# The second experts' stage of a graph-network kernel: row gathers, weight loads, column widths and the last two units rearranged

## The chip, the cores and the metric

The kernel runs on one core of a Trainium2 chip. The time is device time in microseconds (us) of one execution; a kernel's time is the median of several runs. All times of one execution below are counted from the start of its span.

## What is computed

The reference is two rounds of graph aggregation plus attention, each followed by a mixture of experts, over 1250 nodes of 1024 features. The change touches only the last step, the second mixture:

```
scores = einsum('btd,ed->bte', x, gate_w)            # 8 experts
topk_scores, topk_idx = top_k(scores, 2)
topk_probs = softmax(topk_scores)
h1, h2 = split(einsum('btd,ehd->bteh', x, w12))      # 256 + 256 columns per expert
hidden = silu(h1) * h2
expert_out = einsum('bteh,edh->bted', hidden, w3)
y = sum over the two chosen experts of probability * expert_out
```

The kernel's output is x + y, where x in y is the layer-normed x.

## The kernel before, in words

Everything but the last stage is the same in both kernels and is left out here. The framework in which it is written records the instructions, lets a scheduler order them per engine by its own estimates, and inserts the semaphores; a block under a condition is scheduled as one piece.

The last stage computes only what the routing chose. Each node's two experts are known only on the chip, so the nodes of an expert are packed into **units** of up to four blocks (UC = 4) of 128 nodes. There are NU = 12 units; the first five are always run, the others only if their count is at least 1. Lines 1151 to 1296 work out, on the chip, for every unit the expert (`unit_e`), the number of nodes (`taken`), the row numbers for gathers (`idx`, for whole rows of the first unit; `idx_q`, for quarters of rows of the others; `idx_s`, for scatters) and the weights (`gate`).

For one unit the work is:

- **weights** (`load_unit`, L1304): w12 (2 MB) and w3 (1 MB) of its expert, from SyncE's DMA queue for units from 3 on and the first load of unit 0, from ScalarE's queue for units 1 and 2. Each has three buffers.
- **rows**. For unit 0, GpSimd gathers whole rows, 128 at a time (L1320, tile `xe`), TensorE transposes them (L1342) and ScalarE and VectorE in turn evict them (L118 and L120, called by `evac`) into `xeT`. For the other units, GpSimd gathers quarters of rows (`fetch`, L1345 to L1356, tile `xq`, two buffers, four gathers for a block of 128 nodes), and VectorE turns them into `xeT` (`turn`, L1374).
- **gate and up** (`gate_up`, L1381 to L1392), twice, once for each 128 of the 256 hidden columns: 8 matmuls into `p1`, 8 into `p2`, Silu on ScalarE (L1389), the product on VectorE (L1390) into `hT` (named `h3T`), and a memset of the rest of a block of 128 (L1392).
- **down** (L1398 to L1418): for each block, four matmuls (L1406), the eviction with the weight (L1409 on ScalarE, L1411 on VectorE, tile `ye`), and a scatter that adds the rows to the output in memory (L1412, GpSimd).

How many columns a matmul has depends on the unit's count, which is known only at run time. `by_width` (L193) therefore writes the work out once for each width, as the **arms** of a binary tree of jumps, and every engine jumps by the count that it loaded (L1323, `number`). Gate and up had seven arms (L53: 128, 192, 256, 320, 384, 448, 512 columns), rows and down have four (L54, `COUNTS`: 128, 256, 384, 512).

The loop (L1360) runs over the units: in unit u it states the fetch of unit u + 2, the weights of u + 1, gate and up, the turn of u + 1, and down. A unit from 5 on stands under its own condition (`when`, L1328). So three queues matter: GpSimd's, which holds gathers and scatters in one order, ScalarE's, which holds evictions and the weights of units 1 and 2, and SyncE's. The order on each is the scheduler's: in the kernel before, GpSimd has the fetch of unit 1, one row gather of unit 0, the fetch of unit 2, the three other row gathers, the fetch of unit 3, the scatters of unit 0, and from there mostly a fetch and a scatter in turn; the fetches of units 8 and 9 stand behind the scatters of units 5 and 6.

Of the kernel before, what the change touches and what calls it, by code (L numbers as in the profile page):

```python
# [22 lines left out]
P = 128  # L23
N = 1250
D = 1024
KB = D // P
# [23 lines left out]
UC = 4  # L50
NU = 12
COLS = NU * UC
WIDTHS1 = [128, 192, 256, 320, 384, 448, 512]  # L53
COUNTS = [P * (c + 1) for c in range(UC)]  # L54
LN_EPS = 1e-5
EXACT = 4096.0
# [48 lines left out]
def network(tc: tile.TileContext, a: dict, out: bass.AP, env: SimpleNamespace, exact: bool):  # L105
    nc = tc.nc
    wpool, small, psum = env.wpool, env.small, env.psum
    ident, eps_t, iota8 = env.ident, env.eps_t, env.iota8
# [6 lines left out]
    def evac(dst, src):  # L115
        turn[0] += 1
        if turn[0] % 2:
            nc.scalar.copy(dst, src)  # L118
        else:
            nc.vector.tensor_copy(dst, src)  # L120

    def bank(name):
        return psum.tile([P, 512], F32, name=name, tag="bank")
# [69 lines left out]
    def by_width(n, widths, work):  # L193

        if len(widths) == 1:
            return work(widths[0])
        m = len(widths) // 2
        with tc.If(n <= widths[m - 1]) as cmp:
            by_width(n, widths[:m], work)
        with cmp.Else():  # L200
            by_width(n, widths[m:], work)
# [106 lines left out]
    with tc.tile_pool(name="edges", bufs=1, side="right") as edp, \  # L308
# [5 lines left out]
        with tc.tile_pool(name="mix0k", bufs=1, side="right") as kp, ExitStack() as s_edges:  # L314
            blocks = iter(())
            for half in range(2):
# [40 lines left out]
                coming = iter([(pair, j) for pair in range(4) for j in range(nj)])  # L357
# [92 lines left out]
    with tc.tile_pool(name="wo0", bufs=1) as bp:  # L450
# [21 lines left out]
        if not exact:  # L472
            most1 = bp.tile([P, 1], F32, name="most1")
            nc.vector.tensor_reduce(most1, most, AX.X, OP.max)
            pt = bank("pmost")
# [6 lines left out]
    if not exact:  # L482
        with tc.tile_pool(name="deg", bufs=1) as dp:
# [7 lines left out]
            pt = bank("pdc")  # L491
# [78 lines left out]
    hn, b = gcn_features(0)  # L570
# [5 lines left out]
    hn, b = gcn_features(1)  # L576
# [5 lines left out]
    taken = rp.tile([1, E], I32, name="taken")  # L582
    with tc.tile_pool(name="route0a", bufs=1) as ra, tc.tile_pool(name="route0w", bufs=2) as rw:
# [175 lines left out]
        pt = bank("ptab")  # L759
# [22 lines left out]
        pt = bank("pspread")  # L782
# [21 lines left out]
    with s_route:  # L804
        quarters = x1n_d.rearrange("n (j f) -> (n j) f", j=4)
        with tc.tile_pool(name="moe0", bufs=1) as mp:
# [45 lines left out]
            xeT = first_columns()  # L852
            ws = weights(0)

            number = [nc.values_load(taken[0:1, e:e + 1], min_val=0, max_val=CAP) for e in range(E)]
# [445 lines left out]
    with tc.tile_pool(name="moe1", bufs=2) as ep:  # L1301
        SP, ACT = mybir.EngineType.SP, mybir.EngineType.Activation

        def load_unit(w, which, queue):  # L1304
            queue.dma_start(w[0], a["L1_ffn_w12"][bass.ds(which, 1)].rearrange("e (p k) f -> p (e k) f", k=KB))
            queue.dma_start(w[1], a["L1_ffn_w3"][bass.ds(which, 1)].rearrange("e (k p) f -> p (e k) f", p=P))

        def places():
            return (wpool.tile([P, KB, 2 * H1], F32, name="w12", tag="w"),
                    ep.tile([P, H1 // P, D], F32, name="w3", bufs=3))  # L1310

        def expert_of(u, engine):
            return nc.values_load(unit_e[0:1, u:u + 1], engines=(engine,), min_val=0, max_val=E - 1)

        ws = places()
        load_unit(ws, expert_of(0, SP), nc.sync)

        xe = ep.tile([P, UC, D], F32, name="xe1", bufs=1)
        for c in range(UC):
            nc.gpsimd.indirect_dma_start(  # L1320
                out=xe[:, c], out_offset=None, in_=env.x3n_d,
                in_offset=bass.IndirectOffsetOnAxis(ap=idx[:, c:c + 1], axis=0))
        number = [nc.values_load(taken[0:1, u:u + 1], min_val=0, max_val=UC * P) for u in range(NU)]  # L1323

        queues = [(nc.sync, SP) if u > 2 else (nc.scalar, ACT) for u in range(NU)]
        which = [None] + [expert_of(u, queues[u][1]) for u in range(1, NU)]

        def when(u, work):  # L1328

            if u < 5:  # L1330
                return work()
            with tc.If(number[u] >= 1):
                work()

        xeT = ep.tile([P, KB, UC * P], F32, name="xeT1")

        def turn_first(n):
            for c in range(n // P):
                for b0 in (0, 4):
                    pt = bank("pte1")  # L1340
                    for b in range(4):
                        nc.tensor.transpose(pt[:, b * P:(b + 1) * P], xe[:, c, b0 + b::KB], ident)  # L1342
                    evac(xeT[:, b0:b0 + 4, c * P:(c + 1) * P], pt.rearrange("p (b q) -> p b q", b=4))

        def fetch(u):  # L1345
            xq = ep.tile([P, UC * 4, B, KB], F32, name="xq1")

            def work(n):
                for i in range(n // B):
                    nc.gpsimd.indirect_dma_start(  # L1350
                        out=xq[:, i].rearrange("p c b -> p (c b)"), out_offset=None, in_=quarters3,
                        in_offset=bass.IndirectOffsetOnAxis(
                            ap=idx_q[:, i % 4, u * UC + i // 4:u * UC + i // 4 + 1], axis=0))

            when(u, lambda: by_width(number[u], COUNTS, work))
            return xq  # L1356

        by_width(number[0], COUNTS, turn_first)
        coming = [fetch(1)]
        for u in range(NU):  # L1360
            later = u + 1 < NU
            if u + 2 < NU:
                coming.append(fetch(u + 2))
            if later:
                xq = coming.pop(0)
                xeT2 = ep.tile([P, KB, UC * P], F32, name="xeT1")
                ws2 = places()
            w12, w3 = ws
            hT = ep.tile([P, H1 // P, UC * P], F32, name="h3T")

            def turn(n):
                for c in range(n // P):
                    i0, i1 = 4 * c, 4 * c + 4
                    nc.vector.transpose(xeT2.rearrange("p b (i r) -> p i b r", r=B)[:, i0:i1],  # L1374
                                        xq[:, i0:i1].rearrange("p i c b -> p i b c"))

            def unit():
                if later:
                    when(u + 1, lambda: load_unit(ws2, which[u + 1], queues[u + 1][0]))
                for i in range(H1 // P):  # L1380
                    def gate_up(n):  # L1381
                        m = -(-n // P) * P
                        p1, p2 = bank("p1"), bank("p2")
                        for pw_, off in ((p1, 0), (p2, H1)):
                            for k in range(KB):
                                nc.tensor.matmul(pw_[:, :n], w12[:, k, off + i * P:off + (i + 1) * P], xeT[:, k, :n],  # L1386
                                                 start=(k == 0), stop=(k == KB - 1))
                        sg = ep.tile([P, UC * P], F32, name="sg1")
                        nc.scalar.activation(sg[:, :n], p1[:, :n], AF.Silu)  # L1389
                        nc.vector.tensor_mul(hT[:, i, :n], sg[:, :n], p2[:, :n])  # L1390
                        if n < m:
                            nc.vector.memset(hT[:, i, n:m], 0.0)  # L1392

                    by_width(number[u], WIDTHS1, gate_up)
                if later:
                    when(u + 1, lambda: by_width(number[u + 1], COUNTS, turn))

                def down(n):  # L1398
                    sent = []
                    for c in range(n // P):  # L1400
                        ye = ep.tile([P, D], F32, name="ye1", bufs=6)
                        own = gate[:, u * UC + c:u * UC + c + 1]
                        for half in range(2):
                            py = bank("py1")
                            for i in range(H1 // P):
                                nc.tensor.matmul(py, hT[:, i, c * P:(c + 1) * P], w3[:, i, half * 512:(half + 1) * 512],  # L1406
                                                 start=(i == 0), stop=(i == H1 // P - 1))
                            if half:
                                nc.scalar.activation(ye[:, 512:], py, AF.Copy, scale=own)  # L1409
                            else:  # L1410
                                nc.vector.tensor_scalar(ye[:, :512], py, own, None, op0=OP.mult)  # L1411
                        add = nc.gpsimd.indirect_dma_start(  # L1412
                            out=out, out_offset=bass.IndirectOffsetOnAxis(
                                ap=idx_s[:, u * UC + c:u * UC + c + 1], axis=0),
                            in_=ye, in_offset=None, bounds_check=N - 1, oob_is_err=False, compute_op=OP.add)
                        for other in sent:
                            tc.declare_no_dep(add.ins, other.ins, reason="no token is twice at an expert")
                        sent.append(add)  # L1418

                by_width(number[u], COUNTS, down)  # L1420

            when(u, unit)
            if later:
                xeT, ws = xeT2, ws2
    s_moe.close()


# [47 lines left out]
```

## Time and profile before

| what | value |
|---|---|
| median of 3 runs | 3457.25 us (3454.84 to 3459.14) |
| the profiled execution | 3460.19 us |
| its span | 3458.5 us |
| TensorE busy | 3249.1 us, 94% |
| GpSimd busy | 635.5 us, 18% |
| VectorE busy | 941.7 us, 27% |
| end of the routing work (`idx_q`, L1289) | 3110.5 us |
| first gate matmul (L1386) | 3152.0 us |
| last down matmul (L1406) ends | 3433.6 us |
| gate and up matmuls, idle before them for "issue" | 16.8 us |
| down matmuls, idle before them for "issue" | 8.9 us |

In the profile's groups a line has: source line, engine, operation, output and inputs, shapes and count; then busy time and mean ns of one; then the engine's idle time just before and what ended it. "PE" is TensorE, "DVE" VectorE, "ACT" ScalarE, "POOL" GpSimd. "issue" is time in which an engine waited for nothing that the profile shows. In the chain and the timeline a line begins with its start and its length in us. An fp32 matmul of the program shows as two records.

### The profile page before, as it was taken

The page shows a single profiled execution, that of the slowest core. Times are in us where ns is not written, and L with a number is a line of the kernel's source. Part 1 is how long each engine was busy: PE and PEld are TensorE (multiplying, and loading weights), DVE is VectorE, ACT ScalarE, POOL GpSimd, SP SyncE. Part 2 cuts the span into 40 slices and gives each one's busy share as a digit, 9 for nine tenths or more (in the row PEclk, how much of TensorE's full clock was granted, in tenths as well). Part 3 has the DMA queues.
Part 4 walks back from the last instruction along what each step waited for, and adds up shares of the span by engine and source line. Part 5 has one row for each costly group of instructions (what it writes and reads, how often), then busy time and mean ns, then how long its engine had stood idle before and what let it go on. Part 6 is the DMA issues. An engine that isn't in the chain of part 4 may idle for free.

```text
span 3458.5 us, 30927 instructions
## 1 busy us (share of the span) xinstructions
PE 3249.1 (94%) x11696; PEld 1969.2 (57%) x11696; DVE 941.7 (27%) x2405; ACT 358.1 (10%) x622; POOL 635.5 (18%) x543
## 2 busy tenths in 40 slices
PE   6999999999999699999699999999999999986887
PEld 3474656554557466756355555447777454653553
DVE  4248335531114623231520000111111111341221
ACT  1001011100004111111110011000000000000000
POOL 0006786042001041210200000110000010005431
PEclk9999999999998599999899999999999999987998
DMA  4715222054104155554620000220100110236652
GB/s 154 170 58 131 25 1 25 25 182 149 47 31 152 48 185 189 168 182 118 217 101 25 25 25 25 91 108 1 35 15 25 61 48 18 97 119 197 186 171 51
DMA packets 147616, 317.95 MB, mean 92 GB/s; under 512 B 38951, under 2 KB 60366, under 8 KB 143884
## 3 DMA queue, kind: packets, MB, share of 16 engines
q1 hardware_dynamic: 82108, 216.85, 18.4%
q0 software_dynamic: 40240, 48.25, 7.0%
q10 hardware_dynamic: 24992, 49.16, 4.7%
q8 instruction: 174, 2.85, 0.3%
q14 instruction: 102, 0.84, 0.1%
HBM read 239.25 MB, written 77.82 MB: 92 GB/s over the span
## 4 chain that ended last, share of the span: by engine, by line
PE 52%; DMA 2%; issue 1%; DVE 1%; ACT 0%; POOL 0%; another core or an unknown queue 0%; POOLq 0%; DVEq 0%; ACTq 0%; SPq 0%
PE ppn L166 8%; PE pqT L941 8%; PE pa L515 5%; PE p L1386 5%; PE ph L166 4%; PE pwo L166 4%; PE ph L1065 4%; PE pv L166 3%; PE py L1406 2%; PE py L889 2%; PE pgate L869 2%; PE pup L869 2%; PE psc L1083 1%; DMA res_d<-xt 1%; PE pkv L1000 1%
## 5 line engine op out<-in xcount | busy, mean ns | idle before, releaser
L277 POOL DMA_INDIRECT adj_d<-cnt,cell x167 | 261.3, 1565 | 91.9 <-issue 41.7
L1386 PE MATMUL p<-xeT,w 128*128 128x384 f32 (+4 forms) x640 | 167.6, 425 | 18.0 <-issue 16.8
L190 POOL TENSOR_TENSOR xr<-xr,bo 128x512 f32<-128x512 f32 (+1 forms) x40 | 50.4, 1264 | 711.9 <-PE pwo L166 453.5
L1386 PEld LDWEIGHTS p<-xeT,w 128*128 128x128 f32 x640 | 113.8, 201 | 73.9 <-issue 35.5
L869 PE MATMUL pgate<-xeT,wg 128*128 128x392 f32 (+3 forms) x512 | 152.4, 452 | 2.7 <-DVE ye L892 2.5
L166 PE MATMUL pqk<-wk,x0T 128*128 128x512 f32 (+1 forms) x320 | 144.8, 607 | 9.2 <-ACT x0T L118 6.9
L889 PE MATMUL py<-hT,wdb 128*128 128x392 f32 (+3 forms) x512 | 145.8, 444 | 4.1 <-ACT wdb L879 4.0
L166 PE MATMUL pv<-wv,x1T 128*128 128x512 f32 (+1 forms) x320 | 144.3, 609 | 4.2 <-ACT x1T L118 2.2
L869 PE MATMUL pup<-xeT,wu 128*128 128x392 f32 (+3 forms) x512 | 148.2, 443 | 0.0
L166 PE MATMUL ph<-ws,h1T 128*128 128x512 f32 (+1 forms) x320 | 143.2, 596 | 0.0
L166 PE MATMUL pqk<-wq,x0T 128*128 128x512 f32 (+1 forms) x320 | 140.7, 594 | 0.0
L166 PE MATMUL ppn<-wn,x1T 128*128 128x256 f32 (+1 forms) x640 | 138.8, 379 | 0.0
L1065 PE MATMUL ph<-x1T,ws 128*128 128x416 f32 (+1 forms) x384 | 138.2, 512 | 0.0
L166 PE MATMUL pv<-wv,x0T 128*128 128x512 f32 (+1 forms) x320 | 138.0, 593 | 0.0
L166 PE MATMUL ph<-wgcn,x0T 128*128 128x512 f32 (+1 forms) x320 | 138.0, 593 | 0.0
L166 PE MATMUL pwo<-wo,attn0T 128*128 128x512 f32 (+1 forms) x320 | 137.7, 593 | 0.1
L166 PE MATMUL ppn<-wn,h1T 128*128 128x512 f32 (+1 forms) x320 | 137.7, 592 | 0.0
L166 PE MATMUL pwo<-wo,attn1T 128*128 128x512 f32 (+1 forms) x320 | 137.5, 593 | 0.0
L941 PE MATMUL pqT<-x1T,wk 128*128 128x416 f32 (+1 forms) x384 | 135.6, 512 | 0.0
L941 PE MATMUL pqT<-x1T,wq 128*128 128x416 f32 (+1 forms) x384 | 135.6, 512 | 0.0
L166 PEld LDWEIGHTS ppn<-wn,x1T 128*128 128x128 f32 (+1 forms) x640 | 120.1, 188 | 17.7
L869 PEld LDWEIGHTS pgate<-xeT,wg 128*128 128x128 f32 x512 | 99.4, 195 | 50.5 <-issue 6.4
(384 smaller groups left out, 4474.8 us busy)
## 6 DMA issues: line engine op xcount, KB each, us to landing
wg<-in_L_ffn_gate_w_dram SPq DMA_DIRECT2D x8, 2048.0 KB
wu<-in_L_ffn_up_w_dram SPq DMA_DIRECT2D x8, 2048.0 KB
w<-in_L_ffn_w_dram SPq DMA_DIRECT2D x8, 2048.0 KB
wd<-in_L_ffn_down_w_dram SPq DMA_DIRECT2D x7, 2048.0 KB
y_d<-ye ACTq DMA_DIRECT2D x30, 416.0 KB
adj_d<-ezero SPq DMA_DIRECT2D x2, 6105.0 KB
res_d<-xr SPq DMA_DIRECT2D x45, 256.0 KB
table<-adj_d ACTq DMA_DIRECT2D x36, 312.5 KB
```

Of the source, the lines that this page charges most:

```text
L166: nc.tensor.matmul(pr[:TS[t], :cols], xT[:, k, TOK[t]], w[:, k, :], start=(k == 0), stop=(k == nk - 1))
L190: nc.gpsimd.tensor_add(xr[:TS[t]], xr[:TS[t]], bias[:TS[t]])
L277: nc.gpsimd.indirect_dma_start(out=adj_d[e % 2], out_offset=bass.IndirectOffsetOnAxis(ap=cell[:, e:e + 1], axis=0), in_=cnt[:, e:e + 1], i ...
L515: nc.tensor.matmul(pa, edges if by_node else feats, feats if by_node else edges, start=(s == 0 and i == 0), stop=(s == T - 1 and i == len( ...
L869: nc.tensor.matmul(pw[:, :n], w[:, k, ic], xeT[:, k, :n], start=(k == 0), stop=(k == KB - 1))
L889: nc.tensor.matmul(py[:, :n], wdb[:, i, b, :], hT[:, i, :n], start=(i == 0), stop=(i == I0 // P - 1))
L941: nc.tensor.matmul(pq[:, :n], w[:, k, pair * P:(pair + 1) * P], xT[:, k, c0:c0 + n], start=(k == 0), stop=(k == KB - 1))
L1000: nc.tensor.matmul(pkv[:, :P], kf[:TS[t], t, :], v[:TS[t], t, pair * P:(pair + 1) * P], start=(t == 0), stop=(t == T - 1))
L1065: nc.tensor.matmul(ps[:, :n], w[:, k, q0 + f * P:q0 + (f + 1) * P], xT[:, k, c0:c0 + n], start=(k == 0), stop=(k == KB - 1))
L1083: nc.tensor.matmul(pl[:ts, :E], xnt[:, k, :ts], gw[:, k, :], start=(k == 0), stop=(k == KB - 1))
L1386: nc.tensor.matmul(pw_[:, :n], w12[:, k, off + i * P:off + (i + 1) * P], xeT[:, k, :n], start=(k == 0), stop=(k == KB - 1))
L1406: nc.tensor.matmul(py, hT[:, i, c * P:(c + 1) * P], w3[:, i, half * 512:(half + 1) * 512], start=(i == 0), stop=(i == H1 // P - 1))
```

## The change

It has four parts, all in the last stage.

1. Every weight load of a unit is kept in program order, which bars the scheduler from moving it ahead. The load of the counts (`number`) on GpSimd is put behind the last row gather of unit 0, and with it all fetches.
2. The rows of unit 0 are always turned in all four blocks, not by the count.
3. Gate and up use the four widths of `COUNTS` in place of the seven, so hT is always filled to a whole block and the memset goes.
4. The loop becomes a function. Unit 11 stands inside unit 10's condition, so that one jump passes both.

```
-WIDTHS1 = [128, 192, 256, 320, 384, 448, 512]
...
         def load_unit(w, which, queue):
-            queue.dma_start(w[0], a["L1_ffn_w12"][bass.ds(which, 1)].rearrange("e (p k) f -> p (e k) f", k=KB))
-            queue.dma_start(w[1], a["L1_ffn_w3"][bass.ds(which, 1)].rearrange("e (k p) f -> p (e k) f", p=P))
+            for part, name, order in ((w[0], "w12", "e (p k) f -> p (e k) f"), (w[1], "w3", "e (k p) f -> p (e k) f")):
+                tc.keep_in_program_order(queue.dma_start(
+                    part, a["L1_ffn_" + name][bass.ds(which, 1)].rearrange(order, p=P)))
...
         for c in range(UC):
-            nc.gpsimd.indirect_dma_start(
+            whole = nc.gpsimd.indirect_dma_start(
...
-        number = [nc.values_load(taken[0:1, u:u + 1], min_val=0, max_val=UC * P) for u in range(NU)]
+        with tc.issue_after(whole.ins):
+            number = [nc.values_load(taken[0:1, u:u + 1], min_val=0, max_val=UC * P) for u in range(NU)]
...
-        def turn_first(n):
-            for c in range(n // P):
-                for b0 in (0, 4):
+        for c in range(UC):
+            for b0 in (0, 4):
...
-        by_width(number[0], COUNTS, turn_first)
-        coming = [fetch(1)]
-        for u in range(NU):
+        def units_from(u, xeT, ws, coming):
...
                     def gate_up(n):
-                        m = -(-n // P) * P
...
-                        if n < m:
-                            nc.vector.memset(hT[:, i, n:m], 0.0)
-
-                    by_width(number[u], WIDTHS1, gate_up)
+
+                    by_width(number[u], COUNTS, gate_up)
...
                 by_width(number[u], COUNTS, down)
 
+                if later and u == NU - 2:
+                    units_from(u + 1, xeT2, ws2, coming)
+
             when(u, unit)
-            if later:
-                xeT, ws = xeT2, ws2
+            if later and not (u == NU - 2):
+                units_from(u + 1, xeT2, ws2, coming)
+
+        units_from(0, xeT, ws, [fetch(1)])
```

In the changed program GpSimd has the four row gathers first, then the fetches of units 1, 2 and 3; from there its order is as before. ScalarE has unit 1's w12 behind its last row eviction, unit 1's w3 behind the first Silu of unit 0, unit 2's w12 behind the second, and unit 2's w3 behind unit 0's evictions. VectorE turns unit 1 between the two products of unit 0, where it did so ahead of both.

More of the change, by code (lines that the diff above doesn't have):

```diff
@@ L1335, in network @@
         xeT = ep.tile([P, KB, UC * P], F32, name="xeT1")
-        def turn_first(n):
-            for c in range(n // P):
-                for b0 in (0, 4):
[L1340 to L1343, printed above, removed]
+        for c in range(UC):
+            for b0 in (0, 4):
+                pt = bank("pte1")
+                for b in range(4):
+                    nc.tensor.transpose(pt[:, b * P:(b + 1) * P], xe[:, c, b0 + b::KB], ident)
+                evac(xeT[:, b0:b0 + 4, c * P:(c + 1) * P], pt.rearrange("p (b q) -> p b q", b=4))
         def fetch(u):
```

## The prediction

> **What bounds the kernel now.** The page's slices come first: TensorE is busy nine tenths of nearly every slice, but the last five of 40 (from 3026 us) show 8, 6, 8, 8 and 7.
>
> ```profile
> PE   6999999999999699999699999999999999986887
> PEclk9999999999998599999899999999999999987998
> ```
>
> The granted clock falls there too. Next, the chain that ended last, in order of time, through the stage that the diff touches (columns: start, length, what):
>
> ```profile
> 3126.25 2.93 issue
> 3129.18 0.23 POOLq L1323
> 3129.41 10.78 DMA xe<-x3n_d,idx
> ...
> 3143.41 5.58 DMA xe<-x3n_d,idx
> 3149.03 1.99 PE pte L1342 x8
> ...
> 3151.99 17.46 PE p L1386 x64
> 3169.45 10.36 PE py L1406 x24
> ...
> 3275.70 3.57 PE p L1386 x32
> 3279.27 4.04 issue
> 3283.31 5.47 PE p L1386 x32
> ```
>
> Two things are seen. The first gate matmul waits for the first unit's rows until 3151.99, though their indices (L1274) are ready at 3108.50: GpSimd first issues twelve fetches of unit 1 (from 3111.48), then one row gather, eight fetches of unit 2, and three more row gathers. From then TensorE carries the chain to 3433.6, but in narrow units it stops for "issue", and the half of matmuls after such a stop runs slow (5.47 against 3.57). Third, the groups by shape, which give the widths that ran:
>
> ```profile
> L1386 PE MATMUL p<-xeT,w 128*128 128x384 f32 x256 | 83.7, 487 | 2.9 <-issue 2.9
> L1386 PE MATMUL p<-xeT,w 128*128 128x448 f32 x64 | 24.2, 539 | 0.0
> L1386 PE MATMUL p<-xeT,w 128*128 128x192 f32 x128 | 23.1, 343 | 5.3 <-issue 5.0 <-DVE ye L1411 0.3
> L1386 PE MATMUL p<-xeT,w 128*128 128x128 f32 x128 | 19.0, 320 | 8.8 <-issue 8.8
> L1386 PE MATMUL p<-xeT,w 128*128 128x320 f32 x64 | 17.5, 434 | 1.0 <-DVE xeT L120 1.0
> ```
>
> A unit has 64 of these, so by the timeline units 0 to 9 run 320, 384, 192, 448, 128, 384, 192, 128, 384, 384 columns; units 10 and 11 are empty. The timeline also gives the side path of the second half, from GpSimd's fetch for unit 8 to its matmuls:
>
> ```profile
> 3340.41 0.94 POOL L1350 DMA_INDIRECT xq<-x3n_d,idx_q  x1 [5.06 <-DMA out_dram<-ye,idx_s]
> ...
> 3357.54 5.83 DVE L1374 STREAM_TRANSPOSE xeT<-xq 128x1024 f32<-128x1024 f32 x3 [0.77 <-DMA xq<-x3n_d,idx_q]
> ```
>
> **Rows first.** In the changed program's order GpSimd issues the four row gathers before it loads any count. It is idle then (its wait for idx_q is 27.9 us), so they start at about 3108.7 and take 4 x 1.25 us (0.95 and 0.30 of issue). In the trace a row gather reaches the transposes 4.5 to 5.6 us after its start, and a second of the same burst 2.2 us later (3146.83, 3149.03); so the fourth is there at 3108.7 + 4.7 + 3 x 2.2 = 3120.0. It is turned in 2.0 and evicted in 0.7, with 0.5 of issue: the first gate matmul at 3123.2. This contains the fourth block, now always turned (2.2 us). Bounds: 3120 if GpSimd's pace alone counts, 3128 if weights of unit 0 slow the gathers. **-28.8**.
>
> What is moved behind: unit 1's fetches now start at 3114.2 instead of 3111.48, are issued by 3129 and turned by 3140.5; unit 1 needs them at 3154.6. Unit 2's are turned by 3149.5, and unit 0's DVE evictions wait for that, 5.4 us after the down matmuls start; in unit 1 the like wait was 8.7 us (3201.5 to 3210.2) and cost TensorE 0.27. On ScalarE's queue unit 1's w12 moves from 3100.8 to behind the last row eviction (3122.5), its w3 and unit 2's w12 behind unit 0's two Silus (3128 and 3139), and unit 2's w3 behind unit 0's evictions (3154). Unit 3's w12, issued at 3169.49, has its last packet by 3178, so 8.5 us each: unit 1's is there 20 us early. On SyncE unit 0's w3 moves ahead of two branch trees. All at nothing; without that cover each us late is a us.
>
> **Four widths.** 320 becomes 384, 192 becomes 256 twice, 448 becomes 512. 64 matmuls of 384 take 20.9 us, of 448 24.05, of 320 17.46, so 64 columns cost 3.5: units 0, 2, 3, 6 pay 14.1 in all. The eight memsets (0.11 each) leave VectorE, off the path: 0.
>
> **What the fewer arms give back.** Without stops and at full clock (5.36 for 32 of 192, 3.73 for 32 of 128, 0.442 for a down matmul) units 2, 4, 6, 7 would take 17.8, 11.0, 17.8, 11.0 us; they took 25.5, 22.4, 23.4, 19.6: 33 us over. Two jumps explain it. I count the built programs' TensorE instructions (one fp32 matmul is two loads and two multiplies: 640 records for 320 matmuls). An arm is 64 of them, and from one half's arm to the next half's it was some 400 instructions, now some 200. In the trace's branch records 14 of 18 jumps of 350 and more last 1.2 to 6.5 us, and none of the 12 shorter ones lasts over 0.45. After the change the longest jump that runs is 333, the others 304 at most. Wide units hid most of it (5.93 us showed as 0.81 in unit 1).
>
> [...]
> Unit 1 -0.8; unit 2 from 25.5 to 17.8 + 3.5 + 0.5 = 21.8: -3.7; unit 4 from 22.4 to 14.0: -8.4; units 0 and 3 +3.5 each; unit 5 unchanged.
>
> **What is late next.** Units 6 and 7 could lose 10, but unit 8's rows are fetched behind unit 5's scatter-adds. From unit 5's end (3329.4) the fetch ends at +23.2, the rows are turned from +28.1 to +34.0, and nothing in that is TensorE's. VectorE does that turn between unit 7's two products (the order is kept), so unit 7's down matmuls follow it (4 us, clock low again) and unit 8 starts at +38.5, against +43.0: **-4.5**. Unit 9's rows (turned at +60.7 in the trace) then meet unit 8's second product at +59.4: unit 8 gives back 1.0 net of its 0.5 stop. Unit 9: 0.
>
> **One jump.** At the end GpSimd, which finishes last, skips unit 10, adds to its semaphores, skips unit 11 and does so again: 1.8 us between in its records, now gone; TensorE's two skips (3.4 and 5.5 us) lie beside that. **-1.8**.
>
> Sum: -28.8 + 3.5 - 0.8 - 3.7 + 3.5 - 8.4 - 4.5 + 1.0 - 1.8 = -40.0. Against the profiled execution, 3460.19 (span 3458.5 and 1.7 around it), that is 3420; it lies 2.9 above the median of 3457.25, so the median becomes 3417, and I say 3418.
>
> **Rivals.**
> 1. [...] 14%.
> 2. Stops gone wholly, and the fetch chain of unit 8 gives way, since scatter and fetch meet less traffic (5.06 of it was a wait for a landing). Then units 4, 6 and 7 give 2.6 and 6 more, with 1.0 in unit 8: 3407. 18%.
> 3. [...] 3%.
> That the rows do not go ahead is ruled out by the order of GpSimd's instructions.
>
> **Numbers.** The likeliest case, 3418, has 62%, with 3409 to 3429 of its own (3 us on the rows, 4 on the stops, 3 on unit 8). 3% lie near the old time. A measurement tells some 0.2%, 7 us, from no change. The range 3402 to 3438 takes in the likeliest case and the second rival and leaves out the first and third. Faster 94%, same 3%, slower 3%.
>
> **What would show it.** First gate matmul near 3123 (right if 3120 to 3128); only shapes 128, 256, 384, 512 in the gate row; its "issue" idle near 5 instead of 16.8; unit 4 in about 14 us; unit 8's start 38 to 39 us after unit 5's end, with its turn just before. Wrong if the chain shows issue gaps of 4 us in units 4 and 7, or a weight load ahead of unit 1.

## The result and the profile after

| what | before | after |
|---|---|---|
| median of the runs, same chip | 3457.57 us (4 runs) | 3425.07 us (4 runs, 3415.3 to 3425.5) |
| ratio, 95% interval | | 0.990 (0.9881 to 0.9919) |
| profiled execution, its span | 3460.19, 3458.5 | 3425.42, 3423.7 |
| index cast (`idx`, L1274 / L1273) | 3108.3 | 3103.1 |
| index cast to first gate matmul | 43.7 | 15.0 |
| index cast to the end of the span | 350.2 | 320.6 |

The change saves 32.5 us. The prediction said 39 to 40. In the slices of the span (tenths, 40 slices) the last five of TensorE now read 9, 6, 9, 8, 7:

```profile
PE   6999999999999789999699999999999999996987
PEclk9999999999998689999899999999999999997998
```

The groups by shape show the four widths and what TensorE still waits for ahead of them:

```profile
L1383 PE MATMUL p<-xeT,w 128*128 128x384 f32 x320 | 108.7, 502 | 9.2 <-DVE ye L1406 5.3 <-issue 3.9
L1401 PE MATMUL py<-w,h3T 128*128 128x512 f32 x200 | 91.4, 611 | 7.1 <-DVE h3T L1387 6.3 <-issue 0.8
L1383 PE MATMUL p<-xeT,w 128*128 128x256 f32 x128 | 28.1, 380 | 0.6 <-DVE ye L1406 0.6
L1383 PE MATMUL p<-xeT,w 128*128 128x512 f32 x64 | 27.6, 592 | 0.0
L1383 PE MATMUL p<-xeT,w 128*128 128x128 f32 x128 | 14.6, 275 | 0.0
```

"issue" idle is 3.9 for gate and up (16.8 before) and 0.8 for down (8.9 before). In its place stand two waits for VectorE that were not there: 5.3 for `ye` and 6.3 for `h3T`. TensorE's timeline says where (start, length, what, in brackets the idle time before it):

```profile
3118.14 20.81 PE L1383 MATMUL p<-xeT,w 128*128 128x384 f32 x64
3138.78 10.60 PE L1401 MATMUL py<-w,h3T 128*128 128x512 f32 x24
3154.69 23.53 PE L1383 MATMUL p<-xeT,w 128*128 128x384 f32 x64 [5.31 <-DVE ye L1406]
...
3251.52 7.31 PE L1383 MATMUL p<-xeT,w 128*128 128x128 f32 x64
3258.66 3.60 PE L1401 MATMUL py<-w,h3T 128*128 128x512 f32 x8
3266.12 22.42 PE L1383 MATMUL p<-xeT,w 128*128 128x384 f32 x64 [3.86 <-issue]
...
3335.02 5.49 PE L1401 MATMUL py<-w,h3T 128*128 128x512 f32 x6 [6.34 <-DVE h3T L1387]
3340.30 21.11 PE L1383 MATMUL p<-xeT,w 128*128 128x384 f32 x64
```

Each wait costs twice: 64 matmuls of 384 columns take 20.81 undisturbed, but 23.53 behind the wait of 5.31 and 22.42 behind that of 3.86, and six down matmuls take 5.49 where 2.65 is their pace. The granted clock gives the sizes: it was 0.73 of full speed in the 10 us from 3154.69 (2.7 us lost), 0.84 in the 10 us from 3266.12 (1.6) and 0.50 over those six down matmuls (2.6), and 1.00 in the undisturbed 20.81. VectorE's timeline has the cause of the first wait:

```profile
3139.06 0.55 DVE L1387 TENSOR_TENSOR h3T<-sg,p 128x384 f32<-128x384 f32 x1 [1.31 <-PE p L1383]
3142.77 2.03 DVE L1372 STREAM_TRANSPOSE xeT<-xq 128x1024 f32<-128x1024 f32 x1 [3.15 <-DMA xq<-x3n_d,idx_q]
3150.68 2.01 DVE L1372 STREAM_TRANSPOSE xeT<-xq 128x1024 f32<-128x1024 f32 x1 [5.88 <-DMA xq<-x3n_d,idx_q]
3152.61 2.03 DVE L1406 TENSOR_SCALAR ye<-py,gate 128x512 f32<-128x512 f32 x3
```

Unit 0's three evictions (`ye`) stand behind the turn of unit 2, which waits for rows twice (3.15, 5.88). They start 13.8 us after the down matmuls, and unit 1's first matmul waits for them. That it waits for the PSUM tiles which they empty (the matmuls' outputs take turns in eight of them, `bank`) is read from the program; the profile names only `ye`. GpSimd had fetched these rows late:

```profile
3125.05 0.95 POOL L1350 DMA_INDIRECT xq<-x3n_d,idx_q  x1 [0.31 <-issue]
3130.97 0.94 POOL L1350 DMA_INDIRECT xq<-x3n_d,idx_q  x1 [4.98 <-DMA xq<-x3n_d,idx_q]
3132.35 0.94 POOL L1350 DMA_INDIRECT xq<-x3n_d,idx_q  x1 [0.44 <-issue]
```

After unit 1's twelve fetches it waits 4.98 us for a landing before it starts on unit 2's eight. The kernel before had such a wait behind the same twelve fetches, and then took 1.37 us for each of the eight instead of 1.25:

```profile
3125.30 0.95 POOL L1350 DMA_INDIRECT xq<-x3n_d,idx_q  x1 [0.30 <-issue]
3129.41 0.94 POOL L1320 DMA_INDIRECT xe<-x3n_d,idx  x1 [3.16 <-DMA xq<-x3n_d,idx_q]
```

From first gate matmul to first gate matmul (the two profiles' timelines, us; unit 9 to the end of its down matmuls, which before is 3435.3; the 3433.6 of the first table is where the chain leaves TensorE):

| | before | after | difference | predicted |
|---|---|---|---|---|
| index cast to unit 0 | 43.7 | 15.0 | -28.6 | -28.8 |
| unit 0 | 27.7 | 36.6 | +8.9 | +3.5 |
| unit 1 | 32.6 | 34.6 | +2.0 | -0.8 |
| unit 2 | 25.3 | 20.8 | -4.5 | -3.7 |
| unit 3 | 38.0 | 41.5 | +3.5 | +3.5 |
| unit 4 | 22.5 | 14.6 | -7.9 | -8.4 |
| unit 5 | 31.2 | 32.7 | +1.5 | 0 |
| units 6 and 7 | 43.0 | 41.5 | -1.5 | -4.5 |
| unit 8 | 31.8 | 31.4 | -0.4 | +1.0 |
| unit 9 | 31.3 | 31.2 | 0 | 0 |
| to the end | 23.2 | 20.8 | -2.4 | -1.8 |
| stage | 350.2 | 320.6 | -29.6 | -40.0 |

The other 5.2 us of the profiles' difference lie ahead of the index cast, where both kernels have the same instructions. Four kernels of sets three and four (below), with the same work there, have the cast between 3102.6 and 3110.2, so this is scatter and no part of the change. In sets one and two it comes at 3114.3 to 3124.6.

### The profile page after: what moved, and what is told of

Read it like the earlier page. It is cut to its first block, busy times and chain, and to the rows that moved or that the text cites. A ratio compares the mean times of both kernels' runs of the same rounds, so it can differ in the third digit from the quotient of the medians.

```text
span 3423.7 us, 30825 instructions
## 1 busy us (share of the span) xinstructions
PE 3254.8 (95%) x11704; PEld 1966.0 (57%) x11704; DVE 941.5 (27%) x2398; ACT 359.2 (10%) x623; POOL 635.7 (19%) x543
## 5 line engine op out<-in xcount | busy, mean ns | idle before, releaser
L1383 PE MATMUL p<-xeT,w 128*128 128x384 f32 (+3 forms) x640 | 179.0, 442 | 9.8 <-DVE ye L1406 5.9
```

## The experiments

There were four sets of runs, each on one chip with the kernel before beside it: the first on one chip, the second and third on another, the fourth on a third. In the first two sets the kernel before took 3487.2 and 3483.6 us, in the last two 3459.0 and 3460.3. In the first two every profile shows long waits that the others lack (below, "The standstill"); times are compared only within a set, or between sets three and four and the recorded runs.

**Rows first, alone** (set 1; the kernel before with these edits):

```
-        number = [nc.values_load(...) for u in range(NU)]
+        with tc.issue_after(whole.ins):
+            number = [nc.values_load(...) for u in range(NU)]
...
-        by_width(number[0], COUNTS, turn_first)
```

and the weights in program order and all four blocks of unit 0 turned, as in the change.

> The kernel before with the first two parts of the change alone: rows ahead of fetches and weights, four blocks always turned; seven widths and two jumps stay. Theory: the first gate matmul comes 15 us after the index cast in place of 43.7, so 28.6 are gained there; VectorE's turn of unit 2 (late rows) again stands ahead of unit 0's evictions and, as unit 0 is 3.5 us shorter at 320 columns, TensorE waits 5 to 9 us for ye; the issue stops of units 2, 4 and 7 stay. So 3434 to 3438, first gate matmul 28 to 29 earlier against the index cast. Rival (the wait for ye belongs to the wider columns or to the shorter code, not to the order of the rows): no wait for ye, and the whole 28.6 is seen: 3429.

Measured: 3466.7, ratio 0.9944 (0.9925 to 0.9964). TensorE had turned the rows 17 us behind the index cast (43 in the kernel with one jump alone, same set), but then stood still for 18.2 us:

```profile
3127.55 3.92 PE L1343 MATMUL pte<-ident,xe 128*128 128x128 f32 x19 [0.35 <-issue]
3149.68 20.24 PE L1386 MATMUL p<-xeT,w 128*128 128x320 f32 x64 [18.21 <-issue]
```

Neither theory had this, and neither is settled here: with such a standstill in front, the rows had time to come, and no wait for `ye` is longer than 0.28. That the kernel is 20.5 us below the one before, about what the theory said, is luck, since 18.2 us of standstill are in it and others in its neighbour. The stops of units 2, 4 and 7 stayed, as the theory said.

**Four widths, alone** (set 1):

```
-                    by_width(number[u], WIDTHS1, gate_up)
+                    by_width(number[u], COUNTS, gate_up)
```

> The kernel before with the four widths alone. Theory (stops sit on jumps between arms that are far apart): units 0 and 3 +3.5 each, unit 2 25.4 to about 21, unit 4 22.4 to about 14.5, units 6 and 7 together 43.0 to about 41.5, no wait for ye over 1 us: -6 to -8 in all, 3450. Rival (the stops stay however long the jumps are): 14 more columns' time and no gain, 3471. A second rival (nothing but the wait for the rows at the stage's start and GpSimd's chain sets the end, so that shorter units are waited away): within 3 us of before.

Measured: 3467.7, ratio 0.9946 (0.9928 to 0.9964), so 12 to 25 us less: more than the theory, far from both rivals. Against the kernel with one jump alone, from the same set, unit 2 takes 21.7 for 26.2, unit 3 41.5 for 38.0, unit 4 14.7 for 21.8, and units 6 and 7 42.2 for 49.2. The last pair is what the expectation missed: it had been sized by the stops of one profile (43.0), and stops vary.

**The changed columns with the long code** (set 1, and again in set 2):

```
                     def gate_up(n):
+                        n = -(-n // P) * P
...
-                    by_width(number[u], COUNTS, gate_up)
+                    by_width(number[u], WIDTHS1, gate_up)
```

> The changed kernel with the seven-armed tree, but every arm rounded up to whole blocks of 128 columns: the columns computed are those of the changed kernel, the length of the code and of its jumps that of the kernel before. Theory: the stops come back with the length alone: issue idle of the gate row from 4 to about 15 us, unit 2 from 20.9 to 26 or 29, unit 4 from 14.5 to about 22, unit 8 starts up to 1.5 later; 3437 to 3444. Rival (the stops went for another cause than the length of the jumps): 3425, issue idle near 4.

Measured in set 1: 3473.1, ratio 0.997 (0.9959 to 0.9982), with a standstill of 20.7 us again. So it was run beside the changed kernel itself:

> The changed kernel once more, beside the others of this call. In the two runs with seven arms and the rows first, TensorE stood still for 18 and 21 us between the last row transpose and the first gate matmul, with no cause in the profile, though the rows were there. Theory A (the standstill belongs to the long code): none here, first gate matmul 14 to 16 us behind the index cast, ratio to before 0.990. Theory B (it belongs to the chip or the hour, on which the kernel before also took 30 us more): the standstill is here too, first gate matmul 33 to 37 us behind the index cast, ratio 0.994 to 0.997.

> The changed kernel's columns with the seven-armed code once more, beside the changed kernel itself. Theory A (the standstill ahead of the first gate matmul belongs to the long code): it comes again, about 20 us, on top of some 15 us of stops in units 2 and 4; 30 to 36 us above the changed kernel. Theory B (chip or hour): as the changed kernel there, and only the stops, 13 to 20 us above it.

Measured in set 2: the changed kernel 3455.9, ratio 0.9924 (0.990 to 0.9947), the same with the long code 3472.6, ratio 0.9969 (0.9958 to 0.998). The standstill is in both (18.8 and 18.7 us), so it does not belong to the long code. What the long code adds is 16.7 us between the medians, within the 13 to 20 expected (the two intervals leave some 7 to 25). Same columns, same place, first with the long code, then as changed:

```profile
3225.37 7.17 PE L1385 MATMUL p<-xeT,w 128*128 128x256 f32 x32 [0.27 <-DVE ye L1408]
3235.73 8.85 PE L1385 MATMUL p<-xeT,w 128*128 128x256 f32 x32 [3.18 <-issue]
...
3295.15 4.63 PE L1385 MATMUL p<-xeT,w 128*128 128x128 f32 x40
3302.76 2.84 PE L1385 MATMUL p<-xeT,w 128*128 128x128 f32 x24 [2.98 <-issue]
3310.26 5.93 PE L1403 MATMUL py<-w,h3T 128*128 128x512 f32 x8 [4.66 <-issue]
3318.93 23.91 PE L1385 MATMUL p<-xeT,w 128*128 128x384 f32 x64 [2.74 <-issue]
```

```profile
3219.85 14.08 PE L1383 MATMUL p<-xeT,w 128*128 128x256 f32 x64 [0.60 <-DVE ye L1406]
...
3282.10 7.31 PE L1383 MATMUL p<-xeT,w 128*128 128x128 f32 x64
3289.24 3.60 PE L1401 MATMUL py<-w,h3T 128*128 128x512 f32 x8
3297.51 22.57 PE L1383 MATMUL p<-xeT,w 128*128 128x384 f32 x64 [4.67 <-issue]
```

Unit 2 takes 28.2 against 20.8, unit 4 23.8 against 15.4. Two things differ: the instructions that are jumped over, and one more level of jumps in part of the tree. TensorE's branch records tell them apart. Over the ten units, the long code has 176 of them, 15 of which last over 1 us (54.0 us together), and the changed kernel 159, of which five do (15.2 us); all others together take 25.5 and 24.0 us. The same holds in every other profile: 14 to 17 long ones (49 to 64 us) where gate and up have seven arms, three to five (10 to 17 us) where they have four. So the stops come from the longer jumps and not from their number.

**One jump, alone** (set 1; the kernel before, its loop made a function as in the change):

```
                 by_width(number[u], COUNTS, down)
 
+                if later and u == NU - 2:
+                    units_from(u + 1, xeT2, ws2, coming)
```

> The kernel before with the last unit inside the condition of the one before it, alone. Theory: GpSimd passes both by one jump after its last scatter, and the time from the last eviction to the end falls by 1.8 to 2.4 us: 3455, below what the comparison can tell, so the profile has to show it: last eviction to end 22.5 in place of 24.9. Rival: the end is set by the landing of the last scatter and not by the jump, and the tail stays 24.9.

Measured: 3483.1, ratio 0.9989 (0.9974 to 1.0003): no difference that the times can tell. From VectorE's last eviction to the end it is 23.3 us, in the two kernels of the set with two jumps 24.6 each, in the other one with one jump 22.1, and 24.9 and 22.5 before and after. So the jump gives 1.3 to 2.5 us; the theory holds, though this kernel itself falls short of its 1.8.

**VectorE's order** (set 2, and again in set 4; the changed kernel with a copy that needs unit 0's `hT` to be free, ahead of the turn of unit 2):

```
                     by_width(number[u], COUNTS, gate_up)
+                    if u == 1:
+                        nc.vector.memset(hTs[0][0:1, 0, 0:1], 0.0)
+                        nc.vector.tensor_copy(xeT2[0:1, 0, 0:1], hTs[0][0:1, 0, 0:1])
```

> The changed kernel, with a tiny copy on VectorE that puts its turn of unit 2's rows behind unit 0's evictions instead of ahead of them. Theory (the 5.3 us for which TensorE waits for ye ahead of unit 1 come from that order alone, since the turn waits for rows that land at about 32 us after the first gate matmul): that wait is under 1 us, unit 1 begins 31 to 32 us after unit 0 instead of 36.6 and its gate half runs in 21 instead of 23.5, so 7 to 8 us less than the changed kernel. Rival (late rows in any order): unit 1's down matmuls or unit 2's gate wait for the turned rows instead, and the time is within 2 us of the changed kernel.

Measured in set 2: 3454.7, ratio 0.9923 (0.9901 to 0.9945), as the changed kernel beside it. That is not the rival's case: in this set the changed kernel has no wait for `ye` ahead of unit 1 at all, since the standstill gave the rows their time (its longest such wait is 0.60, ahead of unit 2). The edit had nothing to take away.

> The kernel with VectorE's turn of unit 2 behind unit 0's evictions once more, hoped to run without the standstill that hid its effect. Theory (the order of VectorE alone makes TensorE wait ahead of unit 1): that wait falls from 5.3 us to under 1, unit 1's gate half runs in 21 us, unit 1 begins 31 to 33 us after unit 0, and nothing is given back in unit 2, whose rows are turned by 38 us after the first gate matmul and needed at 63; stage 312 to 314 us from the index cast, as with no fetch at all, 7 to 8 less than the changed kernel. Rival (as when the fetches were held: the wait only moves to unit 2): a wait for ye of 3 to 5 us ahead of unit 2, stage 318 to 322.

Measured in set 4, without standstill: 3420.4 against 3460.3, ratio 0.9882 (0.9866 to 0.9899). Unit 0 takes 31.1, unit 1 31.8, and the stage 313.7 in place of 320.6:

```profile
3126.20 20.81 PE L1384 MATMUL p<-xeT,w 128*128 128x384 f32 x64
3146.84 10.60 PE L1405 MATMUL py<-w,h3T 128*128 128x512 f32 x24
3157.27 20.80 PE L1384 MATMUL p<-xeT,w 128*128 128x384 f32 x64
3177.91 10.60 PE L1405 MATMUL py<-w,h3T 128*128 128x512 f32 x24
3189.08 14.08 PE L1384 MATMUL p<-xeT,w 128*128 128x256 f32 x64 [0.57 <-DVE ye L1410]
```

No wait between units 0 and 1, no slow half behind it, nothing given back in unit 2. The theory holds by the profile. By the times this kernel is 1.2% below the kernel before; that it is below the changed one (0.990) is not shown, since the intervals overlap.

**The same, and fetches three units ahead** (set 2):

```
-            xq = ep.tile([P, UC * 4, B, KB], F32, name="xq1")
+            xq = ep.tile([P, UC * 4, B, KB], F32, name="xq1", bufs=3)
...
-            if u + 2 < NU:
-                coming.append(fetch(u + 2))
+            if u + 3 < NU:
+                coming.append(fetch(u + 3))
...
-        units_from(0, xeT, ws, [fetch(1)])
+        units_from(0, xeT, ws, [fetch(1), fetch(2)])
```

> The kernel with that order of VectorE, and three buffers for fetched rows in place of two (the first unit's rows share them), so that GpSimd fetches three units ahead: unit 8's fetch then stands behind unit 4's scatters instead of unit 5's. Theory (unit 8's chain of scatter landing, fetch and turn holds unit 7's down matmuls for 6.3 us, and nothing else does): that wait is gone, unit 8 starts 34 to 36 us after the end of unit 5 instead of 41.6, and with the order of VectorE the sum is 13 to 16 us less than the changed kernel. Rival (the turn meets another late scatter or fetch, the scatters then stand behind more fetches): half of it or nothing, and the tail after the last matmul grows.

Measured: 3465.9, ratio 0.9949 (0.9934 to 0.9965), 11 us more than without it. Three things went wrong. A second burst of fetches ran over the end of unit 0's second gate half, whose Silu was let go 9.1 us after its matmuls (below), and the down matmuls waited 9.5 us with it; that the burst held it up is not shown. Unit 4 took 22.0 us instead of 16.1, with five stops of 0.7 to 1.1 us in its second half, the cause of which is open. And at unit 8, the turn no longer waits for rows (0.45 in place of 5.40), but VectorE has it between unit 7's two products:

```profile
3369.14 0.29 DVE L1388 TENSOR_TENSOR h3T<-sg,p 128x128 f32<-128x128 f32 x1 [7.46 <-PE p L1384]
3369.87 5.81 DVE L1373 STREAM_TRANSPOSE xeT<-xq 128x1024 f32<-128x1024 f32 x3 [0.45 <-DMA xq<-x3n_d,idx_q]
3375.60 0.25 DVE L1388 TENSOR_TENSOR h3T<-sg,p 128x128 f32<-128x128 f32 x1
```

The turn of three blocks takes 5.81 us and half a 128-column unit 3.65 on TensorE, so the down matmuls still wait 4.23. Unit 8 starts 39.4 us after unit 5's end, in the changed kernel of the same set 39.7. So the theory fell, and what holds unit 7 here is the turn's place and length, since its rows were there; in the change the late rows add to it (6.34).

**Fetches held until the rows are evicted** (set 3; for units 1 and 2 `behind` is the last column of the evicted rows; VectorE's order as above):

```
-        def fetch(u):
+        def fetch(u, behind=None):
...
+            if behind is not None:
+                nc.gpsimd.tensor_copy(xq[0:1, 0, 0, 0:2], behind)
```

> The changed kernel, with GpSimd's fetches of units 1 and 2 held until all of unit 0's rows are evicted (two tiny copies on GpSimd that read the evicted rows), and with VectorE's turn of unit 2 behind unit 0's evictions. Theory (where TensorE stood still for 18 to 21 us ahead of the first gate matmul, engines saw TensorE's signals only when GpSimd's burst of 20 fetches was over): the burst now begins behind the evictions, the first gate matmul comes 14 to 16 us behind the index cast whatever the chip, and what is left of the burst delays unit 0's products instead, by 5 to 7 us; where the changed kernel has the standstill this is 12 to 16 us less than it, ratio to before 0.988; where it has none, 6 to 8 less by the missing wait for ye. Rival (the standstill has nothing to do with the fetches): first gate matmul 33 us behind the index cast, time as the changed kernel.

Measured: 3429.8, ratio 0.9918 (0.9902 to 0.9935). This set had no standstill, so its main question was not answered. The wait for `ye` moved: 0.82 us ahead of unit 1 (for VectorE's tiny copy), 5.33 for `ye` ahead of unit 2, as the later fetches push the turn of unit 3 (5.81, after a wait of 4.72 for rows) in front of unit 1's evictions. No gain over the change.

**No fetch for units 1 and 2** (set 3, one execution):

```
-            when(u, lambda: by_width(number[u], COUNTS, work))
+            if u in (1, 2):
+                nc.vector.memset(xq, 0.0)
+            else:
+                when(u, lambda: by_width(number[u], COUNTS, work))
```

> The changed kernel without the fetches of units 1 and 2: their rows are replaced by zeros, so GpSimd has no burst while unit 0 begins. Theory (burst holds signals up): no standstill, first gate matmul 14 to 16 us behind the index cast, no wait for ye ahead of unit 1 and none for h3T in unit 0: units 0 and 1 take 31 to 33 us each. Rival (the standstill comes from the weights, the program's pages or the row gathers themselves): 18 us of standstill as before.

Measured: 3422.0, units 0 and 1 31.5 each, together 8.2 us less than in the change: that is what the late rows of unit 2 cost there. The stage is 312.7 in place of 320.6; that this difference, 7.9, is nearly the same is chance, since the other parts differ by up to 1.9 either way. The first gate matmul is 16.9 behind the index cast.

**No weights for unit 2** (set 3, one execution):

```
-                ws2 = places()
+                ws2 = ws if u == 1 else places()
...
-                if later:
+                if later and u != 1:
                     when(u + 1, lambda: load_unit(ws2, which[u + 1], queues[u + 1][0]))
```

> The changed kernel without the weight load of unit 2, which takes unit 1's weights instead (3 MB less moved while unit 2's rows are fetched). Theory of the late rows by traffic: GpSimd's fetch of unit 2 meets 3 MB less, its rows land 4 to 6 us sooner, and VectorE's last turn of unit 2 with them. Rival (the fetch is late by GpSimd's own pace and its ring): its rows land within 1 us of where they landed. A standstill ahead of the first gate matmul is not expected to change by it.

Measured: 3423.1. The last turn of unit 2 ends 33.3 us after the first gate matmul, in the change 34.5. So the theory of traffic, 4 to 6 us, fell; 1.2 is near the rival's 1. What sets GpSimd's wait for a landing between the two fetches stays open: it is 8.71 here, 4.98 in the change and 3.71 in the last kernel of set 4. The wait for `ye` is 2.50 instead of 5.31, half because unit 0's own down matmuls waited 1.41 for `h3T`.

## Why the prediction was right, and where its sum was off

- **Rows first, -28.8**: measured -28.6. The mechanism is the one named, and GpSimd's pace of 1.25 was as written, but two errors cancel, which is luck:

```profile
3106.26 0.99 POOL L1320 DMA_INDIRECT xe<-x3n_d,idx  x1 [27.90 <-issue]
```

  The first gather started 3.2 us behind the index cast and not 0.4: GpSimd's wait ends at 3105.4, behind the cast of `idx_q`, as that of the first fetch did before. From there to the first gate matmul it took 11.9 us and not 14.5, since the blocks came faster than 2.2 us apart (ScalarE's evictions of the four begin 1.64, 1.67 and 0.89 us after one another) and VectorE's last eviction of the fourth block (3118.34) was not waited for.
- **"Unit 2's are turned by 3149.5 ... At nothing."** This step failed. It put the turn 26.3 us behind the first gate matmul, and 9.0 behind unit 1's turn, which is less than eight fetches of 1.25 and leaves no room for a pause, though the trace of before had one of 3.16. It was 34.5 (14.9 behind unit 1's turn), by GpSimd's wait of 4.98 between the two fetches and 1.4 us for each of unit 2's. Unit 0's evictions so came 13.8 us after the down matmuls instead of 5.4. The comparison with the old unit 1, where 8.7 us cost only 0.27, had an end: at 13.8 us the evictions came after unit 1 could have started. The price is 8.0 us, 5.31 of waiting and 2.72 of slow matmuls. Unit 0 (+8.9 for +3.5) and unit 1 (+2.0 for -0.8) are together 8.2 over, most of the 10.4 that the stage lacks. Shown twice: without these fetches, and with VectorE's order turned, both units take 31 to 32.
- **The weights moved behind, "at nothing"**: no wait for a weight stands in TensorE's row, and unit 2's 3 MB left out moved the rows by 1.2 us only. Right.
- **Stops of the long jumps**: units 2 and 4 predicted 21.8 and 14.0, measured 20.8 and 14.6. The longer code alone brings the stops back (28.2 and 23.8 in set 2). Where they go, the prediction's bound of 350 instructions did not carry over: five jumps of the changed kernel, none longer than 333 by its count, still last 1.0 to 5.4 us, and why these five do is not shown by any run here. The rests of stops in the two sums, 0.5 us in unit 2 and 3 in unit 4, were the author's estimate, and no run shows them; in their place unit 2 has no stop in the recorded profile, and unit 4 has one of 3.9 there and of up to 6.0 in others, at the jump to unit 5, which slows unit 5 (+1.5, not costed).
- **Units 6 and 7, -4.5**: measured -1.5 (unit 8 starts 41.5 after unit 5's end, predicted 38.5; in the other sets' kernels with four widths 39.4 to 42.2, with seven 40.7 to 49.2, so single profiles do not settle how much the widths give here). The mechanism is the one named, the turn between unit 7's products; it ended at +36.0 instead of +34.0, since the fetch waited 6.26 for a landing (5.06 before), and the down matmuls behind it took 5.3 instead of 4.
- **One jump, -1.8**: -2.4 here, about -1.3 alone. **Unit 8, +1.0**: -0.4.
- **The rivals**: the stops did not stay (first: rows, widths and the one jump without any gain from the stops, -28.8 + 14.1 - 1.8, would be 3441) nor vanish; the fetch chain of unit 8 did not give way (second), even with rows ahead of time; no wide unit of the recorded profile had a stop of its own (third; in set two's changed kernel unit 1 had one of 0.90): ahead of the 512-column gate matmuls there is no idle time, and 3.86 of the 3.9 us of issue ahead of the 384-column ones stand at the jump to unit 5.

So 10.4 us of the stage's forecast were not there, and 5.2 us of scatter ahead of the stage hid half of it in the profile's span; that part of the closeness is luck.

## The standstill

In sets one and two, on two chips, the profiles name as releaser (what ended a wait) "remote", which no profile of the recorded kernels or of sets three and four does. In the changed kernel of set two, ScalarE's eviction of rows that TensorE had turned by 3133:

```profile
3131.00 0.59 ACT L117 COPY xeT<-pte 128x512 f32<-128x512 f32 x1 [1.88 <-issue]
3151.30 0.59 ACT L117 COPY xeT<-pte 128x512 f32<-128x512 f32 x1 [19.72 <-remote]
```

GpSimd's burst of 20 fetches ran from 3126.20 to 3151.40. With fetches three units ahead a second burst ran from 3152.99 to 3178.8, and ScalarE's second Silu of unit 0, whose matmuls had ended at 3172.1, was let go at 3181.24:

```profile
3156.61 0.49 ACT L1387 ACTIVATE sg<-p 128x384 f32<-128x384 f32 x1 [0.83 <-PE p L1384]
3181.24 0.49 ACT L1387 ACTIVATE sg<-p 128x384 f32<-128x384 f32 x1 [24.14 <-remote]
```

In the kernel with one jump alone the second product of unit 0, whose matmuls had ended at 3183.3, was let go at 3192.31, a burst of 16 having ended at 3189.2. In these three cases an engine that waited for TensorE was let go at, or within some 3 us of, the end of a burst of gathers; but not every such wait lasted to the end, since one eviction on VectorE was let go at 3140.80, in the middle of the first of these bursts. The first mixture, which is the same in all these kernels, has it too: in the changed kernel of set two, seven waits of VectorE (L871, `hT`) that together last 81.8 us end by "remote", each 1.0 to 2.8 us behind the end of a burst of gathers (L827). It is no property of one chip, since the second chip showed it in set two and not in set three. Where it is absent, the same 20 fetches run with a pause behind the twelfth (4.98 us in the change, 8.71 without unit 2's weights, 3.71 in set 4; 4.60 behind the fifteenth where they were held); where it is present, without one (no gap over 0.50 in the changed kernel of set two). What makes it come is open, and the bursts are a coincidence in time, not a shown cause: the run that should have moved the burst away met no standstill.

## What to carry to other kernels

When a step moves a gather later, follow it through every engine that works in order: here the late rows cost nothing to the unit that needed them, but the turn that waited for them (3.15 and 5.88 us) stood ahead of the evictions of unit 0, and TensorE, about to start unit 1, waited 5.31 for these. Arms that are jumped over were not free here: with the same columns, seven arms in place of four cost 16.7 us over ten units, so a finer choice of widths has to earn more than its code costs. Read the pauses of a queue off the trace of before, and not its best pace alone: the 3.16 us were there. And put the price of a wait at its length plus the slow matmuls behind it (5.3 and 2.7, 3.9 and 1.6 here).
